# Normalisation of the incoming sample: four pieces behind products 8 to 11, against one block behind product 10

## The chip, the cores and the metric

The kernel runs on one core of a Trainium2 chip. The time is the device time of one launch in microseconds (us). Engines are called by the profile's names: PE (matrix products; PEld is its weight load), DVE (vector engine), ACT (scalar engine), POOL (GpSimd) and SP (the queue that issues the DMAs). Each engine takes its own instructions strictly in the order written; engines wait for one another through semaphores.

## The reference, cut to what matters

For each of 64 samples (256 tokens, 768 features):

```
h   = max(layernorm(x), 0)                       # normalise
ctx = adj  @ (h @ Wadj.T) / deg                  # aggregate over neighbours
    + adjT @ (h @ Wrev.T) / rdeg
    + h @ Wself.T
out = x + ctx + (terms of the relations)
```

The normalisation is (x - mean) * rstd, cut off below at 0. All arithmetic is in float32.

## The kernel before, in words

The kernel works on one sample per *step*, 64 steps in all. The code is written in the order in which each engine executes it; nothing is rearranged later. In a step three samples are in work: M, whose products with the weights are computed and added to the output; A = M + 1, whose aggregation (`aggregate`, six parts on PE, each followed by a multiplication on DVE) is done; and N = M + 2, which is *incoming*: loaded, its degrees and statistics taken, its normalised values written.

The products: the three 768x768 weights are applied by a scheme of 15 block products (list `ORDER`) in place of 18. Each is twelve matmul passes into a PSUM accumulator ("bank") called `y`, `v`, `x`, `u`, `z`, `w` or `t`, and is followed by one or two *add-outs* (`add_out`, lines 376 and 378), in which DVE adds the bank to or subtracts it from the sample's `x` tile in SBUF. Banks are used again within a step without being cleared: the next product accumulates on what is there, so it must wait until the add-out of the value before has read the bank. In this text products are counted by place, 1 to 15; the index `k` in the code is one less. The places of the second half:

| place | 8 | 9 | 10 | 11 | 12 | 13 | 14 | 15 | 1 of the next step |
|---|---|---|---|---|---|---|---|---|---|
| bank | w | y | x | t | y | x | y | x | y |

So the 14th product (bank `y`) needs the add-out of the 12th, the 13th and 15th (bank `x`) need those of the 10th and 13th, and the first product of the next step needs the add-out of the 14th.

Behind the k-th product and its add-outs the step writes the work for A and N that belongs to that place (`others_of_step`). For N: degrees and statistics behind the fifth product, `spread` (one transposition on PE, two copies on ACT, DMAs that spread the row factors) behind the ninth, `normalise` behind the tenth. In the first two steps everything of A and N comes 8 and 3 places later (`wait`), and what is left over is written behind the 15th product.

`normalise` works on two halves c of the tokens (128 tokens each). For each half there are three instructions: DVE writes `hx` = max(x - mean, 0) (line 309), ACT writes `hi` = hx * rstd in the type fp32r (line 312), DVE writes `lo`, what is missing from `hi` (line 313). Each waits for the one before. `hi`, `lo` and `hx` have one buffer each. POOL forms the sums and differences of blocks that the products take on their left side (line 358).

Of the kernel before, what the change touches and what calls it, by code (L numbers as in the profile page):

```python
# [9 lines left out]
F32 = mybir.dt.float32  # L10
F32R = mybir.dt.float32r
BF16 = mybir.dt.bfloat16
I32 = mybir.dt.int32
AF = mybir.ActivationFunctionType
ALU = mybir.AluOpType
AX = mybir.AxisListType

P = 128
EPS = 1e-5
MEAN, RSTD, RDEG, RRDEG = 8, 9, 10, 11  # L20
# [41 lines left out]
ORDER = (  # L62
    (5, "y", None, ((1, 1, 0),), ()),
    (7, "v", None, ((1, 0, 1, 2),), ()),
    (9, "x", None, ((1, 0, 0),), ("b2-a1",)),
    (15, "u", None, ((1, 1, 1, 2),), ()),
    (10, "z", None, ((1, 1, 2),), ()),
    (11, "w", None, ((-1, 0, 2),), ()),
    (2, "z", 0, ((1, 0, 1),), ("a1+b0+b1",)),
    (3, "w", 1, ((1, 1, 2),), ("a0+a2+b2",)),  # L70
# [11 lines left out]
def kernel(  # L82
# [29 lines left out]
    nc = tc.nc  # L112
    B, L, H = x.shape
    NREL = e_t.shape[1]
    NBASE = NREL // 2
    C = L // P
# [20 lines left out]
    def main_path(main: ExitStack):  # L137
        pool1 = main.enter_context(tc.tile_pool(name="pool1", bufs=1))
# [12 lines left out]
        def load_weights(products):  # L151
            for n in products:
                right = PRODUCTS[n][1]
                k, o = int(right[1]), int(right[2])
                v = (wadj_t, wrev_t, wself_t)[k].rearrange("(f p) o -> p f o", p=P)
                nc.sync.dma_start(W[n], v[:, :, ts(o, NB)])
# [82 lines left out]
        def load(b):  # L239
            s = S[b]  # L240
            s["x"] = pool3.tile([P, C, H], F32, tag="x", name=f"x_{b}")
            nc.sync.dma_start(s["x"], x_v[b])
            s["adj"] = pool1.tile([P, C, 2, L], I32, tag="adj", name=f"adj_{b}")
            nc.sync.dma_start(s["adj"], adj_v[b])

        def load_xt(b):
            s = S[b]
            s["xT"] = pool1.tile([P, F, L], F32, tag="xT", name=f"xT_{b}")
            nc.sync.dma_start(s["xT"], xt_v[b])

        def degrees(b):

            s = S[b]
            s["a"] = pool2.tile([P, C, 2, L], F32R, tag="a", name=f"a_{b}")
            for c in range(C):
                for k in range(2):
                    nc.scalar.activation(
                        s["a"][:, c, k, :], s["adj"][:, c, k, :], AF.Copy, accum_out=tok[b % 2][:, c, 4 - k : 5 - k]
                    )
# [22 lines left out]
        def spread(b):  # L282

            s = S[b]
            v = cols[b % 2]
            pt = ps1.tile([P, P], F32, tag="pt", name=f"pt_{b}")
            nc.tensor.transpose(pt, v.rearrange("p c k -> p (c k)"), ident)  # L287
            s["tokT"] = pool3.tile([P, P], F32R, tag="tokT", name=f"tokT_{b}")
            nc.scalar.activation(s["tokT"], pt, AF.Copy)
            line = pool2.tile([P, P], F32, tag="line", name=f"line_{b}")  # L290
            nc.scalar.activation(line, pt, AF.Copy)
            d = dram.tile([4, C, P], F32, tag="d", name=f"d_{b}")
            for c in range(C):
                nc.sync.dma_start(d[:, c, :], line[c * 64 + MEAN : c * 64 + RRDEG + 1, :])
            s["row"] = pool1.tile([P, 4, L], F32, tag="row", name=f"row_{b}")
            nc.sync.dma_start(
                s["row"].rearrange("p k i -> p (k i)"), d.rearrange("k c p -> (k c p)").partition_broadcast(P)
            )

        def normalise(b):  # L300

            s = S[b]
            v = cols[b % 2]
            s["hi"] = pool1.tile([P, C, H], F32R, tag="hl0", name=f"hi_{b}")
            s["lo"] = pool1.tile([P, C, H], F32R, tag="hl1", name=f"lo_{b}")
            hx = pool1.tile([P, C, H], F32, tag="hx", name=f"hx_{b}")
            for c in range(C):
                rstd = v[:, c, RSTD : RSTD + 1]
                nc.vector.tensor_scalar(  # L309
                    hx[:, c, :], s["x"][:, c, :], v[:, c, MEAN : MEAN + 1], 0.0, op0=ALU.subtract, op1=ALU.max  # L310
                )
                nc.scalar.activation(s["hi"][:, c, :], hx[:, c, :], AF.Copy, scale=rstd)  # L312
                nc.vector.scalar_tensor_tensor(  # L313
                    s["lo"][:, c, :], hx[:, c, :], rstd, s["hi"][:, c, :].bitcast(F32), op0=ALU.mult, op1=ALU.subtract
                )

        def new_left(b):
            S[b]["X"] = pool2.tile([P, F, 3, L], F32, tag="X", name=f"X_{b}")
# [27 lines left out]
        def left_blocks(b):  # L346
            X = S[b]["X"]
            S[b]["L"] = {f"{'ab'[c]}{k}": X[:, :, k, ts(c, P)] for c in range(C) for k in range(3)}
# [38 lines left out]
        def start():  # L387

            order = [n for n, *_ in ORDER]
            order.remove(12)  # L390
            order.remove(14)
            order[6:6] = (12, 14)
            load(0)
            load_xt(0)
            load_weights(order[:2])
            degrees(0)
            statistics(0)
            spread(0)
            load_rows()
            load_weights(order[2:6])  # L400
            load(1)
            load_weights(order[6:])
            normalise(0)
            new_left(0)
            self_features(0)
            for f in range(F):
                aggregate(0, f)
            prepare_rows()
            left_blocks(0)
            for k, name in enumerate(AHEAD):  # L410
                combine_left(0, name, nc.vector if k % 2 else nc.gpsimd)
            load_xt(1)
            combine_weights(10, nc.vector)

        def first_step(k):

            if k == 0:
                turn(12)
                turn(14)
            ahead = {0: (11,), 1: (2,), 2: (3,), 3: (8,), 4: (6,), 5: (4,), 7: (13,), 9: (1,)}  # L420
            for n in ahead.get(k, ()):
                combine_weights(n, nc.vector)
            if k == 2:
                place_rows()
            if k == 5:
                degrees(1)
                statistics(1)
            if k == 6:
                normalise(1)
            if k == 8:  # L430
                spread(1)

        def others_of_step(A, N, k):

            if A is not None:
                if k == 1:
                    new_left(A)
                if 1 <= k <= F:
                    aggregate(A, k - 1)
                if k == 3:  # L440
                    self_features(A)
                    if N is not None:
                        load_xt(N)
            if N is not None:
                if k == 4:
                    degrees(N)
                    statistics(N)
                if k == 8:
                    spread(N)
                if k == 9:  # L450
                    normalise(N)

        def step(t):

            M, A, N = t, t + 1, t + 2
            has_a, has_n = A < B, N < B
            wait = {0: 8, 1: 3}.get(t, 0)
            if has_n:
                load(N)
            banks = {}  # L460
            for k, (n, bank, row, reads, needs) in enumerate(ORDER):
                for name in needs:
                    combine_left(M, name)
                if t == 0:
                    first_step(k)
                start = bank not in banks
                if start:
                    pool, tag = (ps1, bank) if bank in ("x", "y") else (ps3, "q")
                    banks[bank] = pool.tile([P, 512], F32, tag=tag, name=f"{bank}_{M}")[:, :NB]
                product(M, n, banks[bank], start, row)  # L470
                for read in reads:
                    add_out(M, banks[bank], *read)
                for at in range(k, k + 1 if k + 1 < len(ORDER) else k + 4):
                    others_of_step(A if has_a else None, N if has_n else None, at - wait)
                if t == B - 1 and k == 2:
                    flag_others()
                if k == 13:
                    nc.sync.dma_start(out_v[M][:, 0, :], S[M]["x"][:, 0, :])
            if has_a:
                left_blocks(A)  # L480
                for name in AHEAD:
                    combine_left(A, name)
            nc.sync.dma_start(out_v[M][:, 1, :], S[M]["x"][:, 1, :])
# [170 lines left out]
```

## Time and profile before

| what | us |
|---|---|
| median of 3 runs | 3121.15 (3120.66 to 3122.4) |
| the profiled execution, its own time | 3118.01 |
| its span (first to last instruction) | 3116.1 |
| PE busy | 2948.9 |
| DVE busy | 1365.0 |
| POOL busy | 1895.5 |
| ACT busy | 356.2 |

The span is 1.9 us shorter than the profiled execution's own time, and that time is 3.1 us under the median of the runs. Busy times of engines overlap, so they don't add up to the span. In rows of the timeline the columns are: start, duration, engine, line, operation, tile written <- tiles read, count, and in brackets how long the engine was idle before and what released it.

### The profile page before, as it was taken

The numbers are of one execution on the slowest core, as the hardware profiler recorded it, in microseconds if no ns is written. First come the engines' busy times: TensorE is split into PE (matmuls) and PEld (weight loads), VectorE is DVE, ScalarE is ACT, GpSimd is POOL, SyncE is SP. The second block draws the span as 40 slices with busy tenths as digits, with TensorE's granted clock in tenths as the row PEclk, the third lists the DMA queues.
The fourth block names the chain that finished last, engine by engine and source line by source line (L and its number), as shares of the span: only waits on it lengthen the run. The fifth ranks groups of instructions, "written<-read, shape, count | busy, mean of one in ns | idle before, by whom it ended". The sixth has DMA issues, their size and how long they took to land.

```text
span 3116.1 us, 33214 instructions
## 1 busy us (share of the span) xinstructions
PE 2948.9 (95%) x13514; PEld 2547.7 (82%) x13514; DVE 1365.0 (44%) x2526; ACT 356.2 (11%) x845; POOL 1895.5 (61%) x903
## 2 busy tenths in 40 slices
PE   6899999999999999999999999999999999999999
PEld 4788888888888888888888888888888888888888
DVE  7544444444444444444444444444444444444441
ACT  2110110110101101101111011011110110110100
POOL 4756666666566666665665666656656665666563
PEclk8999999999999999999999999999999999999999
DMA  7122121221221221212212212122122121221210
GB/s 247 61 82 78 61 81 63 77 74 62 78 78 61 82 71 69 81 58 75 78 61 82 78 62 81 63 75 73 65 78 78 61 82 66 74 77 62 75 61 21
DMA packets 126052, 233.24 MB, mean 75 GB/s; under 512 B 7092, under 2 KB 68276, under 8 KB 125896
## 3 DMA queue, kind: packets, MB, share of 16 engines
q1 hardware_dynamic: 125896, 231.08, 21.4%
q8 instruction: 108, 1.77, 0.2%
q14 instruction: 48, 0.39, 0.0%
HBM read 180.46 MB, written 50.59 MB: 74 GB/s over the span
## 4 chain that ended last, share of the span: by engine, by line
PE 77%; DVE 17%; ACT 4%; issue 1%; POOL 0%; DMA 0%; ACTq 0%; SPq 0%; DVEq 0%; POOLq 0%
PE y L363 17%; PE x L363 16%; PE pa L337 11%; PE z L363 10%; PE w L363 10%; DVE hx L309 8%; PE u L363 5%; PE v L363 5%; DVE lo L313 5%; ACT hi L312 4%; DVE x L376 2%; DVE x L378 1%; DVE w L182 0%; PE x L368 0%; PE t L363 0%
## 5 line engine op out<-in xcount | busy, mean ns | idle before, releaser
L363 PE MATMUL y<-w,X 128*128 128x256 f32 x2304 | 551.9, 391 | 119.9 <-DVE x L378 119.9
L363 PEld LDWEIGHTS y<-w,X 128*128 128x128 f32 x2304 | 440.1, 195 | 197.9 <-DVE x L378 138.1
L358 POOL TENSOR_TENSOR X<-X 128x768 f32<-128x768 f32 x190 | 344.3, 1812 | 299.0 <-PE pt L287 275.6
L328 POOL TENSOR_TENSOR xT<-xT,row 128x1536 f32<-128x1536 f32 (+1 forms) x128 | 443.1, 3462 | 11.2 <-DMA row<-d 6.2
L337 PE MATMUL pa<-a,hi 128*128 128x512 f32 x768 | 363.9, 474 | 9.9 <-DVE X L342 7.9
L363 PE MATMUL x<-w,a2+b 128*128 128x256 f32 x1536 | 352.6, 379 | 0.0
L363 PE MATMUL x<-w,X 128*128 128x256 f32 x1536 | 352.3, 379 | 0.0
L342 DVE TENSOR_TENSOR X<-pa,row 128x512 f32<-128x512 f32 x384 | 265.1, 690 | 131.8 <-PE pa L337 131.8
L363 PEld LDWEIGHTS x<-w,X 128*128 128x128 f32 x1536 | 286.7, 190 | 40.6 <-POOL X L358 0.3
L363 PEld LDWEIGHTS x<-w,a2+b 128*128 128x128 f32 x1536 | 282.6, 190 | 39.5
L358 POOL TENSOR_TENSOR b2-a<-X 128x768 f32<-128x768 f32 x64 | 117.4, 1834 | 318.0 <-PE v L363 318.0
L337 PE MATMUL pa<-a,lo 128*128 128x512 f32 x768 | 303.8, 396 | 0.5 <-DVE lo L313 0.5
L270 POOL TENSOR_TENSOR cols<-cols,half 128x2 f32<-128x2 f32 x64 | 68.4, 1068 | 384.7 <-DVE cols L269 384.7
L358 POOL TENSOR_TENSOR a2+b<-X,a2+b 128x768 f32<-128x768 f32 x128 | 233.7, 1826 | 60.2 <-PE x L363 56.2
L309 DVE TENSOR_SCALAR hx<-x,cols 128x768 f32<-128x768 f32 x128 | 258.7, 2021 | 0.0
L329 ACT ACTIVATE X<-xT 128x1536 f32<-128x1536 f32 x64 | 94.9, 1483 | 1399.5 <-POOL xT L328 1399.5
L358 POOL TENSOR_TENSOR a2+b<-X 128x768 f32<-128x768 f32 x64 | 162.7, 2542 | 96.0 <-PE x L368 96.0
L313 DVE SCALAR_TENSOR_TENSOR lo<-hx,cols,hi 128x768 fp32r<-128x768 f32 x128 | 156.3, 1221 | 134.0 <-ACT hi L312 134.0
L363 PE MATMUL y<-w,b0+b 128*128 128x256 f32 x768 | 180.8, 386 | 7.2 <-DVE x L378 4.4
L363 PE MATMUL w<-w,X 128*128 128x256 f32 x768 | 178.4, 382 | 7.9 <-DVE x L376 7.9
L363 PE MATMUL w<-w,a1+b 128*128 128x256 f32 x768 | 178.8, 383 | 2.8 <-DVE x L378 2.8
L363 PE MATMUL z<-w,a2+b 128*128 128x256 f32 x768 | 177.8, 382 | 3.0 <-DVE x L376 3.0
(87 smaller groups left out, 4071.2 us busy)
## 6 DMA issues: line engine op xcount, KB each, us to landing
x<-in_x_dram SPq DMA_DIRECT2D x64, 768.0 KB, 4.5
xT<-in_x_t_dram SPq DMA_DIRECT2D x64, 768.0 KB
out_dram<-x SPq DMA_DIRECT2D x128, 384.0 KB, 2.3
adj<-in_adj_dram SPq DMA_DIRECT2D x64, 512.0 KB, 3.5
row<-d SPq DMA_DIRECT2D x64, 512.0 KB, 4.2
w<-in_Wadj_dram SPq DMA_DIRECT2D x6, 768.0 KB
w<-in_Wself_dram SPq DMA_DIRECT2D x5, 768.0 KB
w<-in_Wrev_dram SPq DMA_DIRECT2D x4, 768.0 KB, 10.2
```

Of the source, the lines that this page charges most:

```text
L270: nc.gpsimd.tensor_tensor(v[:, :, RSTD], v[:, :, RSTD], half, op=ALU.pow)
L309: nc.vector.tensor_scalar(hx[:, c, :], s["x"][:, c, :], v[:, c, MEAN : MEAN + 1], 0.0, op0=ALU.subtract, op1=ALU.max)
L312: nc.scalar.activation(s["hi"][:, c, :], hx[:, c, :], AF.Copy, scale=rstd)
L313: nc.vector.scalar_tensor_tensor(s["lo"][:, c, :], hx[:, c, :], rstd, s["hi"][:, c, :].bitcast(F32), op0=ALU.mult, op1=ALU.subtract)
L328: eng.tensor_tensor(v, v, row[:, k : k + 1, :].to_broadcast([P, f1 - f0, L]), op=op)
L329: nc.scalar.activation(s["X"][:, :, 2, :], xT, AF.Relu)
L337: nc.tensor.matmul(pa, s[part][:, c, ts(f, P)], s["a"][:, c, :, :].rearrange("p s i -> p (s i)"), start=(k == 0), stop=(k == 2 * C - 1),)
L342: nc.vector.tensor_mul(s["X"][:, f, 0:2, :].rearrange("p s i -> p (s i)"), pa, s["row"][:, 2:4, :].rearrange("p s i -> p (s i)"))
L358: (eng or nc.gpsimd).tensor_tensor(L[name], L[x], L[y], op=op)
L363: nc.tensor.matmul(ps, l[:, f, :], W[n][:, f, :], start=(start and f == 0), stop=(row is None and f == F - 1), skip_group_check=not start,)
L376: nc.vector.tensor_add(o, o, ps)
L378: nc.vector.tensor_sub(o, o, ps)
```

## The change

`normalise` is cut into pieces and gets the half c and a flag `last`. A piece that isn't `last` writes `hx` and `hi` of a half; a `last` piece writes its `lo`. In the step, the pieces of N stand one each behind products 8, 9, 10 and 11: hx and hi of the first half, lo of the first half, hx and hi of the second, lo of the second. For samples 0 and 1, which are normalised before the steps and within the first step, the order of instructions stays as it was. The loop for what is left over behind the 15th product goes one place further.

```
-        def normalise(b):
+        def normalise(b, c, last):
 
             s = S[b]
             v = cols[b % 2]
-            s["hi"] = pool1.tile([P, C, H], F32R, tag="hl0", name=f"hi_{b}")
-            s["lo"] = pool1.tile([P, C, H], F32R, tag="hl1", name=f"lo_{b}")
-            hx = pool1.tile([P, C, H], F32, tag="hx", name=f"hx_{b}")
-            for c in range(C):
-                rstd = v[:, c, RSTD : RSTD + 1]
+            rstd = v[:, c, RSTD : RSTD + 1]
+            if c == 0 and not last:
+                s["hi"] = pool1.tile([P, C, H], F32R, tag="hl0", name=f"hi_{b}")
+                s["lo"] = pool1.tile([P, C, H], F32R, tag="hl1", name=f"lo_{b}")
+                s["hx"] = pool1.tile([P, C, H], F32, tag="hx", name=f"hx_{b}")
+            hx, hi, lo = (s[n][:, c, :] for n in ("hx", "hi", "lo"))
+            if last:
+                nc.vector.scalar_tensor_tensor(lo, hx, rstd, hi.bitcast(F32), op0=ALU.mult, op1=ALU.subtract)
+            else:
                 nc.vector.tensor_scalar(
-                    hx[:, c, :], s["x"][:, c, :], v[:, c, MEAN : MEAN + 1], 0.0, op0=ALU.subtract, op1=ALU.max
+                    hx, s["x"][:, c, :], v[:, c, MEAN : MEAN + 1], 0.0, op0=ALU.subtract, op1=ALU.max
                 )
-                nc.scalar.activation(s["hi"][:, c, :], hx[:, c, :], AF.Copy, scale=rstd)
-                nc.vector.scalar_tensor_tensor(
-                    s["lo"][:, c, :], hx[:, c, :], rstd, s["hi"][:, c, :].bitcast(F32), op0=ALU.mult, op1=ALU.subtract
-                )
+                nc.scalar.activation(hi, hx, AF.Copy, scale=rstd)
...
-                if k == 9:
-                    normalise(N)
+                if 7 <= k <= 10:
+                    normalise(N, (k - 7) // 2, k % 2 == 0)
...
-                for at in range(k, k + 1 if k + 1 < len(ORDER) else k + 4):
+                for at in range(k, k + 1 if k + 1 < len(ORDER) else k + 5):
```

The order on DVE in a step from the fourth on, before the change, from the add-out of the eighth product to that of the 15th. A row is: line, operation, tile written <- tiles read, shape. `x_4782` is the sample M whose add-outs these are, `x_5228` the incoming sample N, and the letters `w`, `y`, `x`, `t` behind the comma are the banks.

```order
L376 TENSOR_TENSOR x_4782<-x_4782,w_5324 128x256
L376 TENSOR_TENSOR x_4782<-x_4782,y_5232 128x256
L376 TENSOR_TENSOR x_4782<-x_4782,x_5257 128x256
L309 TENSOR_SCALAR hx_5390<-x_5228,cols_109 128x768
L313 SCALAR_TENSOR_TENSOR lo_5389<-hx_5390,cols_109,hi_5388 128x768
L309 TENSOR_SCALAR hx_5390<-x_5228,cols_109 128x768
L313 SCALAR_TENSOR_TENSOR lo_5389<-hx_5390,cols_109,hi_5388 128x768
L378 TENSOR_TENSOR x_4782<-x_4782,t_5398 128x256
L376 TENSOR_TENSOR x_4782<-x_4782,t_5398 128x256
L378 TENSOR_TENSOR x_4782<-x_4782,y_5232 128x256
L378 TENSOR_TENSOR x_4782<-x_4782,x_5257 128x256
```

Four instructions of the normalisation stand in one block ahead of the add-outs of the 11th, 12th and 13th product. The same rows after the change, on DVE (line numbers are those of the changed kernel):

```order
L377 TENSOR_TENSOR x_4782<-x_4782,w_5324 128x256
L313 TENSOR_SCALAR hx_5364<-x_5228,cols_109 128x768
L377 TENSOR_TENSOR x_4782<-x_4782,y_5232 128x256
L311 SCALAR_TENSOR_TENSOR lo_5363<-hx_5364,cols_109,hi_5362 128x768
L377 TENSOR_TENSOR x_4782<-x_4782,x_5257 128x256
L313 TENSOR_SCALAR hx_5364<-x_5228,cols_109 128x768
L379 TENSOR_TENSOR x_4782<-x_4782,t_5397 128x256
L377 TENSOR_TENSOR x_4782<-x_4782,t_5397 128x256
L311 SCALAR_TENSOR_TENSOR lo_5363<-hx_5364,cols_109,hi_5362 128x768
L379 TENSOR_TENSOR x_4782<-x_4782,y_5232 128x256
L379 TENSOR_TENSOR x_4782<-x_4782,x_5257 128x256
```

One instruction of the normalisation stands now between each two groups of add-outs, and the first comes two add-outs earlier than before. On DVE in the second step, where everything of N comes three places later, the rows before are these (M is `x_168`, the last row is the first add-out of the third step):

```order
L378 TENSOR_TENSOR x_168<-x_168,y_549 128x256
L378 TENSOR_TENSOR x_168<-x_168,x_567 128x256
L309 TENSOR_SCALAR hx_733<-x_545,cols_110 128x768
L313 SCALAR_TENSOR_TENSOR lo_732<-hx_733,cols_110,hi_731 128x768
L309 TENSOR_SCALAR hx_733<-x_545,cols_110 128x768
L313 SCALAR_TENSOR_TENSOR lo_732<-hx_733,cols_110,hi_731 128x768
L378 TENSOR_TENSOR x_168<-x_168,y_549 128x256
L378 TENSOR_TENSOR x_168<-x_168,x_567 128x256
L376 TENSOR_TENSOR x_255<-x_255,y_772 128x256
```

The block stands there ahead of the add-outs of the 14th and 15th product. After the change, on DVE in the second step:

```order
L313 TENSOR_SCALAR hx_706<-x_545,cols_110 128x768
L379 TENSOR_TENSOR x_168<-x_168,y_549 128x256
L311 SCALAR_TENSOR_TENSOR lo_705<-hx_706,cols_110,hi_704 128x768
L379 TENSOR_TENSOR x_168<-x_168,x_567 128x256
L313 TENSOR_SCALAR hx_706<-x_545,cols_110 128x768
L379 TENSOR_TENSOR x_168<-x_168,y_549 128x256
L311 SCALAR_TENSOR_TENSOR lo_705<-hx_706,cols_110,hi_704 128x768
L379 TENSOR_TENSOR x_168<-x_168,x_567 128x256
L377 TENSOR_TENSOR x_255<-x_255,y_772 128x256
```

No two instructions of the normalisation stand together there any more. On ACT the rows of a later step before the change, with the two copies of `spread` (lines 289 and 291) and both halves of `hi`:

```order
L257 ACTIVATE a_5304,tok_107<-adj_5230 128x256 x4
L289 ACTIVATE tokT_5371<-pt_5369 128x128
L291 ACTIVATE line_5373<-pt_5369 128x128
L312 ACTIVATE hi_5388<-hx_5390,cols_109 128x768 x2
L329 ACTIVATE X_5471<-xT_5288 128x6x256
```

After the change, on ACT:

```order
L257 ACTIVATE a_5304,tok_107<-adj_5230 128x256 x4
L316 ACTIVATE hi_5362<-hx_5364,cols_109 128x768
L289 ACTIVATE tokT_5376<-pt_5374 128x128
L291 ACTIVATE line_5378<-pt_5374 128x128
L316 ACTIVATE hi_5362<-hx_5364,cols_109 128x768
```

The first `hi` has moved ahead of the two copies of `spread`. On PE, POOL and SP the sequence of instructions is the same as before.

More of the change, by code (lines that the diff above doesn't have):

```diff
@@ L402, in start @@
             load_weights(order[6:])
-            normalise(0)
+            for c in range(C):
+                for last in (False, True):
+                    normalise(0, c, last)
             new_left(0)
@@ L428, in first_step @@
             if k == 6:
-                normalise(1)
+                for c in range(C):
+                    for last in (False, True):
+                        normalise(1, c, last)
             if k == 8:
```

## The prediction

> **What bounds the kernel now.** I read the shares of the span first, then who waits for whom, then one step of the timeline, then the busy time by stretches.
>
> ```profile
> span 3116.1 us, 33214 instructions
> PE 2948.9 (95%) x13514; PEld 2547.7 (82%) x13514; DVE 1365.0 (44%) x2526; ACT 356.2 (11%) x845; POOL 1895.5 (61%) x903
> ```
>
> PE is busy for 95% of the span, so the most that any reordering can bring is its idle time and what comes with that. The chain of waits says who causes it; the columns are total us, times, and the longest:
>
> ```profile
> PE y L363 <- DVE x L378: 124.3, 61, 4.4
> PE pt L287 <- POOL cols L270: 9.1, 1, 9.1
> ```
>
> One wait recurs, 61 times: a product on bank y waits for an add-out on DVE. The next in rank occurs once, at the start. Below is a step in the middle of the run, from the end of the eighth product to the start of the 14th.
>
> ```profile
> 1092.80 2.75 PE L363 MATMUL y<-w,X 128*128 128x256 f32 x12
> 1093.00 0.42 DVE L376 TENSOR_TENSOR x<-x,w 128x256 f32<-128x256 f32 x1 [2.02 <-PE w L368]
> 1095.59 0.42 DVE L376 TENSOR_TENSOR x<-x,y 128x256 f32<-128x256 f32 x1 [2.17 <-PE y L363]
> 1095.70 0.28 ACT L289 ACTIVATE tokT<-pt 128x128 fp32r<-128x128 f32 x1 [12.09 <-PE pt L287]
> 1095.70 1.81 POOL L358 TENSOR_TENSOR X<-X 128x768 f32<-128x768 f32 x1 [4.59 <-PE pt L287]
> 1098.09 2.75 PE L363 MATMUL t<-w,X 128*128 128x256 f32 x12
> 1098.29 0.42 DVE L376 TENSOR_TENSOR x<-x,x 128x256 f32<-128x256 f32 x1 [2.28 <-PE x L363]
> 1098.40 1.80 POOL L358 TENSOR_TENSOR a2+b<-X,a2+b 128x768 f32<-128x768 f32 x1 [0.89 <-PE x L363]
> 1098.63 2.00 DVE L309 TENSOR_SCALAR hx<-x,cols 128x768 f32<-128x768 f32 x1
> 1100.17 2.14 POOL L358 TENSOR_TENSOR b0+b<-X 128x768 f32<-128x768 f32 x1
> 1100.74 0.94 ACT L312 ACTIVATE hi<-hx,cols 128x768 fp32r<-128x768 f32 x1 [4.60 <-DVE hx L309]
> 1101.71 1.41 DVE L313 SCALAR_TENSOR_TENSOR lo<-hx,cols,hi 128x768 fp32r<-128x768 f32 x1 [1.09 <-ACT hi L312]
> 1102.27 2.52 POOL L358 TENSOR_TENSOR a1+a<-X 128x768 f32<-128x768 f32 x1
> 1103.04 2.17 DVE L309 TENSOR_SCALAR hx<-x,cols 128x768 f32<-128x768 f32 x1
> 1103.08 0.47 PE L368 MATMUL y<-rows,tokT 128*128 128x256 f32 x1
> 1103.39 2.75 PE L363 MATMUL x<-w,a2+b 128*128 128x256 f32 x12
> 1105.25 0.94 ACT L312 ACTIVATE hi<-hx,cols 128x768 fp32r<-128x768 f32 x1 [3.57 <-DVE hx L309]
> 1105.79 0.47 PE L368 MATMUL x<-rows,tokT 128*128 128x256 f32 x1
> 1106.21 1.02 DVE L313 SCALAR_TENSOR_TENSOR lo<-hx,cols,hi 128x768 fp32r<-128x768 f32 x1 [1.00 <-ACT hi L312]
> 1107.15 0.41 DVE L378 TENSOR_TENSOR x<-x,t 128x256 f32<-128x256 f32 x1
> 1107.48 0.41 DVE L376 TENSOR_TENSOR x<-x,t 128x256 f32<-128x256 f32 x1
> 1107.81 0.42 DVE L378 TENSOR_TENSOR x<-x,y 128x256 f32<-128x256 f32 x1
> 1108.28 2.86 PE L363 MATMUL y<-w,X 128*128 128x256 f32 x12 [2.02 <-DVE x L378]
> ```
>
> The 12th product is complete at about 1103.55 (1103.08 + 0.47). Its add-out runs at 1107.81, 4.3 us later, since DVE is in the block hx, lo, hx, lo from 1098.63 to 1107.2. The block lasts 8.6 us, though its four instructions are busy for 6.6 (2.00 + 1.41 + 2.17 + 1.02): the rest is DVE waiting for ACT's hi (1.09 and 1.00). PE finishes the 13th product at 1106.26 (1105.79 + 0.47) and then stands until 1108.28: 2.02 us.
>
> By stretches (us; busy time and instructions of each engine; PEclk is the granted TensorE clock, 1.00 being full):
>
> ```profile
> 0.00:151.50 151.50, 114.65 (x456) 92.62 (x456) 101.86 (x143) 29.72 (x63) 84.68 (x44) 0.92 0.48 159
> 151.50:206.20 54.70, 48.31 (x211) 41.54 (x212) 23.83 (x42) 6.34 (x14) 31.91 (x16) 0.94 0.20 71
> 206.20:3024.80 2818.60, 2700.69 (x12451) 2339.39 (x12450) 1220.08 (x2301) 318.69 (x767) 1742.46 (x827) 0.99 0.21 72
> 443.70:492.88 49.18, 47.17 (x213) 40.68 (x212) 20.69 (x39) 5.40 (x13) 30.18 (x15) 0.97 0.21 70
> 492.88:540.40 47.52, 45.50 (x213) 39.45 (x212) 20.70 (x39) 5.40 (x13) 28.93 (x14) 1.00 0.21 73
> 482.29:485.71 3.42, 1.41 (x8) 0.98 (x7) 2.42 (x6) 0.94 (x1) 2.00 (x1) 1.00 0.00 0
> 485.71:489.12 3.41, 3.41 (x8) 2.78 (x9) 0.25 (x1) 0.00 (x0) 3.33 (x3) 0.50 0.00 0
> 489.12:492.53 3.41, 3.41 (x17) 3.02 (x17) 0.42 (x1) 0.00 (x0) 2.64 (x2) 1.00 0.24 98
> ```
>
> Fourth and fifth row: a step takes 47.52 us with 45.50 of PE work, or 49.18 with a piece at half clock. The last three rows place that piece: a stretch in which PE worked for 1.41 of 3.42 us because of the stall, then 3.41 us at 0.50, then full clock again. The third row spans 59 steps, by the count of one product (twelve passes each, 708 / 12); beside it stands the idle time of that stretch:
>
> ```profile
> L363 PE MATMUL y<-w,X 128*128 128x256 f32 x2124 | 510.2, 391 | 117.9 <-DVE x L378 117.9
> L363 PE MATMUL y<-w,b0+b 128*128 128x256 f32 x708 | 162.5, 379 | 0.0
> ```
>
> 2818.60 - 2700.69 is 117.9 too: in these steps PE has no other idle time.
>
> **The change, part by part.** No instruction is added or removed, and the sequences of PE, POOL and SP stay. I replay the step above in the new order, with the same durations.
>
> - *Behind the eighth product:* hx of the first half starts at 1093.4, after the add-out. POOL is idle there (4.59 us up to 1095.70). What hx costs then isn't in this step; over the run it took between these bounds (min/median/max in ns):
>
> ```profile
> L309 DVE TENSOR_SCALAR hx<-x,cols x128: 607/1996/2169, 8.8 to 3014.1; 128x768 f32<-128x768 f32 x128
> ```
>
>   I take 0.61, since both costly cases in the step stand beside POOL's additions; with 2.17 it ends at 1095.6. Then hi is done at 1095.0 (or 1096.6). ACT is idle from long before until 1095.70, so tokT is late by 0.9 us at worst; what follows from it (a transfer for the next step) isn't the releaser of any recurring wait of PE.
> - *Behind the ninth:* add-out until 1096.0, then lo, 1.41 us, until 1097.4 (1098.0 at worst), before the add-out of the tenth can start at 1098.29. Its wait for hi is gone, because hi has the ninth product's time to run.
> - *Behind the tenth:* hx at 1098.63 as now, 2.00 us, hi until 1101.7.
> - *Behind the 11th:* its bank is complete at about 1100.8 (1098.09 + 2.75); two add-outs until 1101.6, lo until 1103.1 (with 1.41).
> - *Behind the 12th:* add-out from 1103.55 to 1104.0. PE wants the bank at 1106.26, so 2.3 us of cover are left. The 2.02 us stall goes entirely. If all the cover were gone, each further us late would cost 1 us in 60 steps.
>
> What is late next: nothing at the 13th and 15th product, whose add-outs (1098.7, about 1106.7) are earlier than their needs (1103.39, and 1106.26 + 2.75 = 1109). POOL starts from PE's events and moves with them; its hx-lengthened additions (2.14, 2.52 against 1.80) only get shorter. It is busy for 28.93 us of a step, so a step of 45.50 leaves it 16 us.
>
> Second step: its block stands ahead of the add-out of the 14th product, which holds up the first product of the third step:
>
> ```profile
> 155.31 0.41 DVE L378 TENSOR_TENSOR x<-x,y 128x256 f32<-128x256 f32 x1
> 155.87 5.46 PE L363 MATMUL y<-w,b0+b 128*128 128x256 f32 x12 [4.37 <-DVE x L378]
> ```
>
> That 4.37 us goes by the same argument, one lo being left ahead of nothing but the last add-out. The 5.46 us in place of 2.75 is half clock again.
>
> **The sum**, against the profiled execution: stalls in the 59 steps 117.9; their half-clock excess 2700.69 - 59 x 45.50 = 16.2; the stretch 151.50 to 206.20, which is one step with both stalls and half clock, 54.70 - 45.50 = 9.2. Together 143.3. Added cost: 0, by the cover of 2.3 us. The rest (0 to 151.50, and 91.3 us after 3024.80) I leave as it is. The span becomes 3116.1 - 143.3 = 2972.8; with 1.9 us around it 2974.7; the median of runs lies 3.1 us over the profiled execution, so 2977.8, say **2978 us** (ratio 0.954).
>
> The half-clock term is the one I had to decide. The row at 485.71 begins as PE resumes, and the stretch ahead of it is the emptiest of its step; I count it as a consequence of the stall. [...] The trace shows the drop right behind 2.0 us, so I go by the trace.
>
> **The rivals.**
>
> 1. *The half-clock stretches have another cause and stay.* For: only about one stall in six is followed by one (16.2 us at 1.66 each, 49.18 - 47.52, is ten in 59 steps), so the stall alone isn't sufficient. Against: the place of the one shown. Time: 2978 + 16.2 + 2.8 (the excess in the second row, 48.31 - 45.50) = 2997. [...] Chance 0.07.
> 2. *The stall stays because DVE's hx is held up by POOL.* The second hx starts beside POOL's run of additions at 1098.40, 1100.17 and 1102.27. Held through one, it takes 2.00. Through two (end 1102.31): hx 1102.9, hi 1103.9, lo 1105.4, add-out 1105.8, still hidden. Only through three (1104.79) would the add-out end at 1108.2 and the whole stall return. Between these, part of it. For: hx is 1.4 us longer beside POOL. Against: it never took more than 2.17. Time 3050 (half) to 3121 (all). Chance 0.06, half of it within 0.2% of before.
> 3. *Slower: a piece blocks the queue in front of the add-outs.* The first lo now stands ahead of the add-out of the tenth product; if hi came late, DVE would hold that add-out, those of the 11th and 12th queue behind, and PE stop before the 13th product at 1103.39. lo would have to end after 1102.9, so hi after 1101.5, against 1095.0 worked out: 6.5 us of cover. It gets slower from 2.4 us beyond that (143.3 / 60), and by 60 us for each further us: with two, 3241. For: hi waits also for PE to have read the old hi and for rstd. Against: both stand ahead of the eighth product in the code, and ACT idles for 12.09 us. Chance 0.03.
>
> That the change doesn't do what it says is excluded by the order of DVE's rows.
>
> **How the numbers follow.** The forecast, 2978, has 0.84. Its own spread: hx and lo change nothing by the cover; the first 151.5 us, with a clock of 0.92, may fall otherwise against the clock by a few us, and the runs lie 2.7 to 4.4 us over the profiled execution; I allow 10 below: 2968. Above, the range takes in the first rival: 2999. That leaves out less than 2 in 10. Faster by over 0.2% (about 6 us, as much as a measurement of this kernel can tell from no change): 0.84 + 0.07 + 0.03 = 0.94; within: 0.03; slower: 0.03.
>
> **What would show it.** In the profile after: PE at about 98% of the span (2948.9 - 19.0 = 2930 of 2973), DVE still at about 44 to 46%; the wait of y's product for line 379 (378 now) gone from the chain of waits; steps of 45.5 us; the granted clock 1.00 in each stretch of the middle; hx's median lower, with half of its instances at about 0.61; ACT's hi still waiting for hx, DVE's lo hardly for hi. The forecast is wrong if a recurring wait of PE for DVE or POOL is left, if steps of 47.2 us (45.50 + 1.66) recur with full PE, or if the add-out of the tenth product comes later than 1.2 us after its bank.

## The result, and the profile after

The changed kernel takes 2961.78 us (2961.04 to 2961.99) against 3121.43: a ratio of 0.949 (95% interval 0.947 to 0.950). Forecast were 2978 with a range from 2968: the sign and the mechanism came as written, but 16 us more were gained, and the time lies 6 us below the range.

The page after, its first lines:

```profile
span 2958.4 us, 33335 instructions
PE 2914.0 (98%) x13514; PEld 2535.1 (86%) x13514; DVE 1368.2 (46%) x2526; ACT 355.9 (12%) x845; POOL 1851.2 (63%) x903
```

The chain of waits of PE (total us, times, longest). The recurring wait of bank y for DVE is gone; what is left occurs once or twice, all of it in the first 117 us but for one wait of 0.6 us near the end. The longest three are:

```profile
PE pt L287 <- DVE cols L280: 11.3, 1, 11.3
PE w L364 <- DVE x L377: 7.8, 1, 7.8
PE pa L338 <- DVE X L343: 7.7, 2, 4.4
```

Busy time by stretches, as before: the start, the third step, the 59 steps from the fourth on (as 206.20:3024.80 before), and one of these steps:

```profile
0.00:153.96 153.96, 115.59 (x456) 93.47 (x457) 106.12 (x145) 30.31 (x64) 85.24 (x44) 0.92 0.49 159
153.96:199.18 45.22, 45.22 (x213) 39.46 (x212) 20.75 (x39) 5.40 (x13) 29.69 (x15) 1.00 0.23 77
199.18:2867.15 2667.97, 2667.97 (x12451) 2328.00 (x12450) 1222.15 (x2301) 318.68 (x767) 1698.40 (x827) 1.00 0.22 76
1058.36:1103.58 45.22, 45.22 (x214) 39.46 (x212) 20.75 (x39) 5.40 (x13) 28.77 (x15) 1.00 0.22 76
```

In 59 steps PE is busy for every microsecond, at full clock. And a step takes 45.22 us, not the 45.50 that I had read as its work.

The same part of a step as in the prediction, after the change:

```profile
1085.07 0.42 DVE L377 TENSOR_TENSOR x<-x,w 128x256 f32<-128x256 f32 x1 [2.02 <-PE w L369]
1085.40 0.61 DVE L313 TENSOR_SCALAR hx<-x,cols 128x768 f32<-128x768 f32 x1
1086.13 0.94 ACT L316 ACTIVATE hi<-hx,cols 128x768 fp32r<-128x768 f32 x1 [10.45 <-DVE hx L313]
1087.66 0.42 DVE L377 TENSOR_TENSOR x<-x,y 128x256 f32<-128x256 f32 x1 [1.64 <-PE y L364]
1087.77 1.81 POOL L359 TENSOR_TENSOR X<-X 128x768 f32<-128x768 f32 x1 [4.59 <-PE pt L287]
1087.99 2.39 DVE L311 SCALAR_TENSOR_TENSOR lo<-hx,cols,hi 128x768 fp32r<-128x768 f32 x1
1090.36 0.42 DVE L377 TENSOR_TENSOR x<-x,x 128x256 f32<-128x256 f32 x1
1090.69 2.00 DVE L313 TENSOR_SCALAR hx<-x,cols 128x768 f32<-128x768 f32 x1
1093.69 1.49 DVE L311 SCALAR_TENSOR_TENSOR lo<-hx,cols,hi 128x768 fp32r<-128x768 f32 x1
1095.15 0.47 PE L369 MATMUL y<-rows,tokT 128*128 128x256 f32 x1
1095.66 0.42 DVE L379 TENSOR_TENSOR x<-x,y 128x256 f32<-128x256 f32 x1 [0.47 <-PE y L369]
1097.86 0.47 PE L369 MATMUL x<-rows,tokT 128*128 128x256 f32 x1
1098.16 2.75 PE L364 MATMUL y<-w,X 128*128 128x256 f32 x12
```

The add-out of the 12th product runs 0.04 us after its bank is complete (1095.15 + 0.47), DVE having even waited for it, where before it was 4.3 us late. No lo waits for hi in this step. The last two rows, both of PE, hold the missing 0.28 us; they are read below.

### The profile page after: what moved, and what is told of

Read it like the earlier page. It is cut to its first block, busy times and chain, and to the rows that moved or that the text cites. A ratio compares the mean times of both kernels' runs of the same rounds, so it can differ in the third digit from the quotient of the medians.

```text
span 2958.4 us, 33335 instructions
## 1 busy us (share of the span) xinstructions
PE 2914.0 (98%) x13514; PEld 2535.1 (86%) x13514; DVE 1368.2 (46%) x2526; ACT 355.9 (12%) x845; POOL 1851.2 (63%) x903
## 4 chain that ended last, share of the span: by engine, by line
PE 96%; DVE 2%; issue 1%; POOL 0%; DMA 0%; ACT 0%; SPq 0%; DVEq 0%; ACTq 0%; POOLq 0%
PE x L364 22%; PE y L364 22%; PE pa L338 12%; PE z L364 11%; PE w L364 11%; PE u L364 6%; PE t L364 6%; PE v L364 5%; PE x L369 1%; PE y L369 1%; DVE w L182 0%; PE z L369 0%; PE w L369 0%; PE pt L287 0%; DVE w L179 0%
## 5 line engine op out<-in xcount | busy, mean ns | idle before, releaser
L364 PE MATMUL y<-w,X 128*128 128x256 f32 x2304 | 528.4, 379 | 0.0
L364 PEld LDWEIGHTS y<-w,X 128*128 128x128 f32 x2304 | 428.4, 190 | 56.5
L311 DVE SCALAR_TENSOR_TENSOR lo<-hx,cols,hi 128x768 fp32r<-128x768 f32 x128 | 242.0, 1891 | 7.3 <-ACT hi L316 7.2
L316 ACT ACTIVATE hi<-hx,cols 128x768 fp32r<-128x768 f32 x128 | 119.8, 936 | 942.6 <-DVE hx L313 942.6
L379 DVE TENSOR_TENSOR x<-x,x 128x256 f32<-128x256 f32 x128 | 54.0, 422 | 289.0 <-PE x L369 289.0
```

The costliest lines, as they stand in the source:

```text
L311: nc.vector.scalar_tensor_tensor(lo, hx, rstd, hi.bitcast(F32), op0=ALU.mult, op1=ALU.subtract)
L316: nc.scalar.activation(hi, hx, AF.Copy, scale=rstd)
L364: nc.tensor.matmul(ps, l[:, f, :], W[n][:, f, :], start=(start and f == 0), stop=(row is None and f == F - 1), skip_group_check=not start,)
L379: nc.vector.tensor_sub(o, o, ps)
```

## The experiments

There were two questions. What in the old block cost the time: the waits of DVE for ACT, the place, or that it was uncut? And to what belongs the 0.28 us per step that my sum missed: to PE's stall (each stall costs more than its idle time), or to the block of normalisation running beside PE?

**The block in another order.** The kernel before, with hx, hx, lo, lo on DVE:

```
             for c in range(C):
                 ...                      # hx, hi
+            for c in range(C):
+                rstd = v[:, c, RSTD : RSTD + 1]
                 nc.vector.scalar_tensor_tensor(...)   # lo
```

> The block stays behind the tenth product, but stands as hx, hx, lo, lo on DVE, so that DVE waits for ACT less. If the waits for ACT and the length of the block are the cause, the block shrinks from 8.6 us to 5.8 to 6.9 us: the add-out of the 12th product ends between 1105.7 and 1106.7 on the clock of the step shown, where PE needs it at 1106.1. Between no stall (2962 us, steps of 45.22) and a stall of 0.6 us (about 3010 us). Rival, the place behind the tenth product is what costs, whatever the waits: still a stall of about 2 us, near 3121 us. On the 0.28 us that each step lost beyond my sum: if it belongs to a stall of PE (what its queue loses by running empty and starting again), a step takes 45.22 without a stall, and 45.22 + idle + 0.27 with one; if it belongs to the block of normalisation running beside PE, a step without a stall still takes 45.5 (2979 us).

Measured: 3037.99 us, ratio 0.974 (0.972 to 0.975), above the range that was expected. One wait of PE, one step, and the block on DVE (hx twice, lo twice):

```profile
PE y L365 <- DVE x L380: 60.1, 61, 4.4
531.29:577.71 46.42, 45.49 (x213) 39.45 (x212) 21.69 (x39) 5.40 (x13) 28.39 (x15) 1.00 0.23 74
517.22 4.09 DVE L309 TENSOR_SCALAR hx<-x,cols 128x768 f32<-128x768 f32 x2
521.23 3.50 DVE L315 SCALAR_TENSOR_TENSOR lo<-hx,cols,hi 128x768 fp32r<-128x768 f32 x2
```

The stall shrinks from 2.02 to 0.93 us (46.42 - 45.49), less than expected, and no half clock is left in the 59 steps (granted clock 1.00). The block now lasts 7.5 us in place of 8.6. DVE's waits for ACT (1.09 and 1.00) are gone, but the two lo take 3.50 us in place of 2.43 (1.41 + 1.02), which I had not reckoned with; why is told with the prices of the pieces below. So without the waits the block alone still holds up the add-out. PE is booked with 45.49 us for the same work that takes 45.22 when nothing stops it.

**Two pieces, waits for ACT kept.** The changed kernel, with the first half behind the ninth product and the second behind the 11th:

```
-                if 7 <= k <= 10:
-                    normalise(N, (k - 7) // 2, k % 2 == 0)
+                if k == 8 or k == 10:
+                    for last in (False, True):
+                        normalise(N, (k - 8) // 2, last)
```

> Two pieces in place of four: the whole first half (hx, hi, lo with DVE's wait for ACT) behind the ninth product, the whole second half behind the 11th. DVE's queue worked out from the rows: the add-out of the tenth product ends at 1101.0 (needed at 1103.1), that of the 12th at about 1106.6 (needed at 1106.1). So a stall of 0 to 0.5 us. If a stall costs its idle time and 0.27 us more: 2962 to 3008 us; if it costs its idle time alone: 2962 to 2992. If the waits for ACT had to go for the gain: near 3121.

Measured: 2962.3 us, ratio 0.949 (0.947 to 0.950): no different from four pieces. DVE still waits for hi in each half, and the add-out of the 12th product (fifth row) stands at the very end of its cover, ending at 556.59 where the product that needs it starts at 556.75. The last row is the 59 steps:

```profile
549.66 2.02 DVE L311 SCALAR_TENSOR_TENSOR lo<-hx,cols,hi 128x768 fp32r<-128x768 f32 x1 [1.08 <-ACT hi L316]
551.60 0.41 DVE L377 TENSOR_TENSOR x<-x,x 128x256 f32<-128x256 f32 x1
552.11 0.42 DVE L379 TENSOR_TENSOR x<-x,t 128x256 f32<-128x256 f32 x1
554.77 1.48 DVE L311 SCALAR_TENSOR_TENSOR lo<-hx,cols,hi 128x768 fp32r<-128x768 f32 x1 [1.00 <-ACT hi L316]
556.18 0.41 DVE L379 TENSOR_TENSOR x<-x,y 128x256 f32<-128x256 f32 x1
200.34:2869.09 2668.75, 2668.73 (x12452) 2327.57 (x12451) 1218.54 (x2301) 318.71 (x767) 1698.04 (x827) 1.00 0.22 76
```

So neither the wait for ACT nor the number of pieces matters in itself, only how late the add-outs come on which PE waits.

**The uncut block at another place**, behind the eighth product:

```
+                if k == 7:
+                    normalise(N)
                 if k == 8:
                     spread(N)
-                if k == 9:
-                    normalise(N)
```

> The uncut block, moved from behind the tenth to behind the eighth product. If only the cutting helps: a stall of about 2 us somewhere, near 3121. If the place is what counts: the block runs from 1093.4 to about 1100.5, partly with POOL idle, and holds up the add-out of the ninth product until 1100.9, which the 12th needs at about 1100.5: a stall of 0.4 to 1 us at the 12th product, 45.9 to 46.5 us a step, 3000 to 3040 us; none at the 14th.

Measured: 3020.39 us, ratio 0.968 (0.966 to 0.969). The stall has moved to the 12th product, which waits for the add-out of the ninth:

```profile
1115.33 1.89 DVE L313 SCALAR_TENSOR_TENSOR lo<-hx,cols,hi 128x768 fp32r<-128x768 f32 x1 [1.00 <-ACT hi L312]
1117.14 0.41 DVE L376 TENSOR_TENSOR x<-x,y 128x256 f32<-128x256 f32 x1
1117.70 2.83 PE L363 MATMUL y<-w,X 128*128 128x256 f32 x12 [0.66 <-DVE x L376]
528.97:575.10 46.13, 45.46 (x214) 39.40 (x212) 19.88 (x39) 5.28 (x13) 28.65 (x15) 1.00 0.21 74
```

The place alone, with nothing cut, brings about two thirds of the gain.

**How much cover the change leaves, and stalls of chosen length.** The changed kernel with n bn_stats (a DVE instruction that gathers statistics) that write a scratch tile, ahead of the add-out of the 12th product:

```
+                if has_n and t >= 2 and k == 10:
+                    for _ in range(n):
+                        nc.vector.bn_stats(pad, S[N]["x"][:, 0, :HO])
```

With n = 4:

> The changed kernel with four bn_stats of 384 elements (0.5 us each, into a scratch tile that nothing reads) on DVE between the pieces behind the 11th product and the add-out of the 12th, in the third to the 62nd step. In the changed kernel DVE is free there from 1140.57 and the add-out has to end by about 1143.2, so the cover is 2.2 us. Expected: 2.0 us of work ahead of the add-out costs nothing, 2962 us, steps of 45.22 us. If cover were gone already: 3080.

Measured: 2960.95 us, ratio 0.949 (0.947 to 0.950). Four instructions more on DVE in each step cost nothing: the cover is there. With n = 8, 9, 10 and 13:

> As with four, but eight bn_stats (4.0 us): the add-out ends at about 1145.0, and PE idles for about 1.5 us before the 14th product in 60 steps. If a stall costs PE's idle time and 0.27 us more, which the profile books as busy: steps of 45.22 + 1.5 + 0.27 = 47.0, 3068 us. If the 0.27 belongs to the normalisation block: steps of 46.7, 3050 us. Half-clock stretches: none if only a stall of about 2 us brings them; about ten, one per 287 us, if they have a cause of their own.

> Nine bn_stats (4.5 us): a stall of about 2.0 us as in the kernel before, without its block of normalisation. If stalls are all that the kernel before lost: steps of 47.5 us and a few half-clock stretches (0 to 15, since 2.0 us is where they set in), 3099 to 3125 us. If the block itself cost 0.27 us: steps of 47.2, 3080 us.

> Ten bn_stats (5.0 us): a stall of about 2.5 us. By the theory that half clock follows a stall of which 2 us fall into one 3.4 us stretch of a fixed grid: steps of 48.0 us and a half-clock stretch more often than in one step of six, 20 to 40 of them at 1.7 us, 3163 to 3197 us. By the rival that they come by themselves at about 287 us: ten, 3146 us. [...]

> 13 bn_stats (6.5 us): a stall of about 4.0 us. [...] By the rival that half clock has a cause of its own: 3220 + 17 = 3237 us.

Measured: 3114.62, 3139.82, 3214.91 and 3389.27 us (ratios 0.998, 0.997 to 0.999; 1.007, 1.005 to 1.008; 1.030, 1.028 to 1.031; 1.086, 1.084 to 1.088). Each bn_stats delays the add-out by 0.6 us and not by the 0.5 assumed, so all stalls came out longer than intended and all four times lie above what was expected. Therefore the step is what is to be read. A step without half clock with n = 8, with 9 and with 10:

```profile
535.81:583.16 47.35, 45.48 (x214) 39.46 (x213) 24.94 (x47) 5.40 (x13) 28.80 (x14) 1.00 0.21 72
536.29:584.24 47.95, 45.48 (x214) 39.45 (x213) 25.51 (x48) 5.40 (x13) 28.81 (x14) 1.00 0.21 72
498.63:547.17 48.54, 45.48 (x214) 39.45 (x212) 26.07 (x49) 5.40 (x13) 28.78 (x14) 1.00 0.21 71
```

Idle times are 1.87, 2.47 and 3.06 us, and PE is booked with 45.48 each time. The normalisation stands in four pieces in all three, so the 0.26 over 45.22 does not belong to its block: it comes with a stall, once, whatever its length, from 0.66 us (the block behind the eighth product, 0.24) to 3.06.

The half clock: over the 59 steps with n = 8, 9, 10 and 13,

```profile
200.97:3020.51 2819.54, 2708.66 (x12451) 2345.28 (x12450) 1469.50 (x2773) 318.58 (x767) 1699.43 (x826) 0.99 0.21 72
198.99:3041.53 2842.54, 2696.56 (x12452) 2336.95 (x12450) 1502.58 (x2832) 318.56 (x767) 1699.50 (x826) 1.00 0.21 72
202.30:3121.48 2919.18, 2738.03 (x12451) 2366.41 (x12450) 1535.66 (x2891) 318.58 (x767) 1699.16 (x826) 0.98 0.20 70
207.02:3296.25 3089.23, 2802.76 (x12452) 2413.18 (x12450) 1634.88 (x3068) 318.59 (x767) 1698.60 (x826) 0.96 0.19 66
```

the excess of PE's busy time over 59 x 45.48 = 2683.3 is 25, 13, 55 and 119 us. These are 15, 8, 34 and 82 stretches at half clock, counted in the traces' records of the clock; the 34 lie within the 20 to 40 expected of the grid, and with n = 13 there is more than one to a stall. A cause of its own, ten stretches whatever the stalls, would give 16 us each time, and the changed kernel, which has none, 16 too. That falls. That 2.47 us costs less than 1.87 looks odd. Three stalls show why. With n = 8 (the stretch with the stall, then the next):

```profile
525.40:528.82 3.42, 1.55 (x8) 1.15 (x7) 3.28 (x7) 0.00 (x0) 1.98 (x2) 1.00 0.00 0
528.82:532.23 3.41, 3.41 (x9) 2.70 (x9) 0.06 (x1) 0.00 (x0) 3.38 (x2) 0.50 0.00 0
```

With n = 9, two stalls, in stretches 3.413 us long that are laid out from the start of the half clock at 338.66 (the second stall is 69 of them on):

```profile
335.24:338.66 3.42, 1.35 (x6) 1.23 (x7) 2.27 (x5) 0.00 (x0) 3.34 (x3) 1.00 0.00 0
338.66:342.07 3.41, 3.41 (x10) 2.69 (x10) 0.32 (x1) 0.00 (x0) 3.33 (x2) 0.50 0.00 0
574.18:577.60 3.42, 2.06 (x10) 1.55 (x9) 3.22 (x6) 0.00 (x0) 1.93 (x2) 1.00 0.00 0
577.60:581.01 3.41, 2.30 (x11) 2.05 (x12) 1.35 (x4) 0.00 (x0) 3.33 (x3) 1.00 0.00 0
581.01:584.42 3.41, 3.41 (x18) 3.05 (x17) 0.42 (x1) 0.00 (x0) 2.54 (x2) 1.00 0.31 120
```

With n = 8 the 1.87 us lie whole in one stretch, and the next is at half clock. With n = 9 the first stall lies with 2.07 us in one stretch, and half clock follows; the second, equally long, is cut by a border into 1.36 and 1.11, and the clock stays. Three stalls alone would not show a grid, but the traces' records of the clock do: with n = 10 the clock drops to half 30 times from 294.6 us on, and each drop lies a whole number of stretches of 3.413 us behind the first, to within 0.005 us over 2915 us. In the kernel before it drops 16 times from 45.39 us on, and each drop lies a whole number of stretches of 3.4133 us behind the first, again to within 0.005 us, over 3069 us.

How much pause is enough can be counted in the 59 steps. In the kernel before, 10 stalls had 2.01 us within one stretch, and half clock followed all of them; the other 49 had at most 1.97 us within one, and it followed none. With n = 9 it followed all 8 stalls with 2.01 us or more within one stretch, and none with less. With n = 8, 18 stalls of 1.87 us lay whole in one stretch, and it followed 15. So in these two kernels half clock followed exactly the stalls with 2.01 us or more of pause within one stretch; why 1.87 us was mostly enough with n = 8, and 1.97 us not in the kernel before, stays open.

## Why the prediction was right or wrong, point by point

- **What bounds the kernel: right.** PE, held up once per step by an add-out behind the block of normalisation. Without the late add-out nothing else recurs.
- **The stalls, 117.9 us: right.** The idle time of PE in the 59 steps is 0.
- **The half clock, 16.2 us, counted as a consequence of the stall: right.** The granted clock is 1.00 throughout the 59 steps, and half clock came back with the stalls that were put in. A stall of 1.87 us was enough in 15 of the 18 cases in which it fell whole into one stretch (n = 8).
- **The clean step, 59 x 45.50: wrong, and this is the error.** I took the PE busy time of a step with a stall, 45.50, for what the step takes without one; it takes 45.22. The difference stands in two rows of PE before the change:

```profile
1105.79 0.47 PE L368 MATMUL x<-rows,tokT 128*128 128x256 f32 x1
1108.28 2.86 PE L363 MATMUL y<-w,X 128*128 128x256 f32 x12 [2.02 <-DVE x L378]
```

 Matmuls overlap. In the changed kernel the next product starts 0.30 us after the start of that 0.47 us matmul (1097.86 to 1098.16), before its booked end; in front of a stall there is nothing to overlap with, which books 0.17 us more. Behind the stall the product's twelve passes take 2.86 in place of 2.75, 0.11 more; why, no run shows. Together 0.28, in 59 steps 16.5 us. The number needed was in the fence that I quoted: the start of the 13th product, 0.31 us after the 0.47 us matmul before it (1103.08 to 1103.39).
- **The sum again.** In the 59 steps 2818.60 - 2667.97 = 150.6: 117.9 + 16.2 + 16.5. The third step gave 54.70 - 45.22 = 9.5 for 9.2. The start came out 2.5 us longer (153.96 for 151.50) where I had left it as it was; PE's first wait is 11.3 us there in place of 9.1, and why is open. The span fell by 157.7 us, where 143.3 were forecast. The median then lay 0.7 us over the profiled execution, not 3.1, which made another 2.4 us of the miss; the execution lay 2.6 us over its span, not 1.9, which took 0.7 off. Together 14.4 + 2.4 - 0.7, the 16 us.
- **The cost of the pieces, 0 by a cover of 2.3 us: right**, with 2.4 us of added work hidden (n = 4). The stalls with n = 8 to 10 grow by 0.6 us for each bn_stats and would reach 0 at about 4.9 of them, 2.9 us; DVE waits 0.47 of that for the bank anyway, so the cover is 2.4 us, an estimate. The first hx took 0.61 us, as chosen. One price inside was off: the first lo takes 2.39 us and not 1.41, and 1096.0 + 2.39 lies past the 1098.29 at which I had the add-out of the tenth product start. Lo's mean over the run rose from 1221 to 1891 ns, and hx's median fell from 1996 to 1158:

```profile
L313 DVE TENSOR_SCALAR hx<-x,cols x128: 608/1158/2437, 9.1 to 2854.3; 128x768 f32<-128x768 f32 x128
L311 DVE SCALAR_TENSOR_TENSOR lo<-hx,cols,hi x128: 1011/1493/2397, 13.1 to 2857.3; 128x768 fp32r<-128x768 f32 x128
```

 The delay of the tenth product's add-out was nothing all the same (1090.36, its bank complete at about 1090.3).

 Both the 1.41 and the 2.39 us were taken beside an addition of POOL's; what differs is how much of that addition was left. The lo of 2.39 us starts 0.22 us after one that ends at 1089.58 (1087.77 + 1.81), and ends at 1090.38, 0.80 us behind it. The lo of 1.41 us, in the kernel before, starts late in one that ends at 1102.31 (1100.17 + 2.14), and ends at 1103.12, 0.81 us behind it. So it is throughout: in the 59 steps of the kernels before and after and of the first three experiments, every lo that starts while an addition runs ends 0.81 to 0.82 us after that addition, and every hx 0.41 to 0.42 us after it (177 lo and 175 hx in the kernels before and after alone). Where none is running at its start, lo takes 1.00 to 1.02 us and hx 0.61 to 0.62. This is also why the two lo with the order hx, hx, lo, lo took 3.50 us. The 1.41 us was therefore a price of that place, not of lo. POOL's two additions that were to get shorter (2.14 and 2.52 us) did not (2.14 and 2.53), which cost nothing.
- **The rivals.** The first (half clock with a cause of its own) did not come: the granted clock is 1.00 in the 59 steps. The second (DVE's hx held up by POOL) did not come: 2.00 us behind the tenth product, as before, held through one addition only. The third (a piece blocking the queue) did not either. The range failed because its lower end was made from the scatter of the start and of the runs only; I gave no bound to the clean step, as if it had been measured.

## What to carry to other kernels

In an engine that takes its instructions in order, cut a block so that each piece fits between two instructions on which the bounding engine waits, and check for each of those how late it may come; the number of pieces doesn't matter once all are in time. When you price the removal of a stall on PE, don't subtract only its idle time (here each stall cost 0.24 to 0.28 us more): find a place in the same trace where the same kinds of product follow each other without a stall, and take start to start. When you move a DVE instruction, price it by what POOL is running at its new place, not by its duration at the old one (the first lo took 1.41 us at the old place and 2.39 at the new). And look at the clock behind a stall before you call it cheap: 1.87 us of stall in each of 59 steps cost 25 us by half clock.

## What the runs showed of the hardware that was not expected

- A stall of PE costs its idle time and about 0.24 to 0.28 us more, which the profile books as busy (45.46 to 45.50 against 45.22, in the kernel before and five others, with stalls of 0.66 to 3.06 us).
- A pause of PE of 1.87 us was followed by 3.41 us at half clock in 15 of 59 steps, and one of 2.47 us in only 8 of 59. The drops of the clock lie on a fixed grid of 3.413 us, and half clock followed the pauses of 2.47 us with 2.01 us or more within one stretch of it, and no other. A stall of 1.87 us in each of 59 steps cost 25 us by half clock, one of 2.47 us 13 us, and one of 4.86 us on average (286.5 / 59, n = 13) 119 us.
- An hx or lo on DVE that started while POOL ran an addition ended 0.41 to 0.42 us (hx) or 0.81 to 0.82 us (lo) after that addition, whatever was left of it. So lo took from 1.41 to 2.57 us in such places in the 59 steps of five kernels, and 1.00 to 1.02 us elsewhere.
